# A routed feed-forward kernel: GpSimd retires its DMAs along the way, one expert's weights load later, and the planner's times change

## The chip, the cores and the metric

The kernel runs on one core of a Trainium2 chip. A core has five engines with their own instruction queues: TensorE (PE in the profile, with its weight loads as PEld), VectorE (DVE), ScalarE (ACT), GpSimd (POOL) and SyncE (SP). SP and ACT issue plain DMAs, on the profile's queues q1 and q10. GpSimd issues the indirect ones, gathers and scatters by a list of row numbers, on q0. All of them are carried out by the core's 16 DMA engines. The time is device microseconds of one execution. Before the change it was 445.34 us, the median of 3 runs (443.35 to 445.86).

## The reference

The inputs are `x` (8 batches of 256 tokens with 256 features), a context of 77 rows for each batch, and a mask.

```
h   = x + layernorm_affine(softmax(mask(LN(x) @ ctx^T / 16)) @ ctx)
out = h + sum over the two best of 8 experts e of
          p_e * ((silu(g_e) * u_e) @ w_down[e]),   [g_e, u_e] = LN(h) @ w_gate_up[e]
```

The two best experts of a token are those with the largest gate probability, `softmax(LN(h) @ w_gate)`, and the two probabilities are scaled to sum to 1. Everything is float32. One expert has 2 MB of gate and up weights (256 x 2048) and 1 MB of down weights (1024 x 256).

## The kernel before

**Two halves.** The first half handles the batches as eight *units* of 256 tokens: attention, the second layer norm, the choice of two experts. Each unit adds its result to `out` (line 816) and stores its normalized rows with gates and expert numbers into a scratch tensor in memory, `xn_rows` (line 850; unit 1 from SP's queue, the others from ACT's). After unit 1, and again after unit 2, a small table of row numbers is made (`first_table`). The second half goes over 29 *tiles* of tokens that belong to one expert (`tile_work`). Tiles 0 to 7 hold the first tokens of the experts 0 to 7, tile 0 from units 0 and 1, the others from units 0 to 2. Tiles 8 to 28 follow a second table and need all units; eight of them are wide, with two groups of rows.

**One tile.** GpSimd gathers the tile's rows from `xn_rows` into one of four buffers `xg` (line 1185, in `pool_rows`). PE transposes them (1264), ACT copies the result (1271), and PE multiplies with the gate and up weights (1314). ACT takes silu (1336), DVE the product (1343), and PE multiplies with the down weights (1375, or 1372 in a wide tile). DVE scales by the gate (1423), and GpSimd adds the rows to `out` with an accumulating scatter (1189). DVE also computes each token's gate from the gathered rows (1278, in `gate`), and the first of these works of tiles 0 and 1 matters below. Each scatter waits for the one before it to have landed. The last tile (28) is different: GpSimd reads the rows that `out` holds by then into `sums` (line 1185 again), DVE adds them in (1421), and the last scatter writes without accumulating.

**Weights.** Three buffers (`LANES = 3`) hold the weights of three experts. `weight_dmas` issues three DMAs on SP for one expert: two halves of `wgu` (line 259) and `wd` (260). The loop at line 284 issues those of experts 0 and 1 at the start of the kernel, behind the inputs. The load for tile 2 waits, through a one-element memset of its buffer (line 1234), for the gate work of tile 1. Later loads wait for the products that last used the buffer.

**The order.** The order on each engine's queue is written by a planner (`class Order`). Every piece of work is entered with an engine, a cost, what it needs, a rank, and a `lag`, the time from its end until others may use its result. The planner walks through time and emits, on each engine, the work that can begin first; among those within `NEAR` of each other it takes the lowest rank. An engine carries out its queue strictly in that order. Work with the engine "in" stands for inputs that arrive at a given time (`c_in`, `x_in`, `m_in_`, `gb_in`, lines 345 to 350). PE's work that begins before `WARM` is planned at 1.9 times its cost. Where the planner sees PE without work ahead of tile 0, it fills the gap with dummy products (`fill`, line 314, line 319 in the profile), at 0.22 us each before `WARM` and 0.12 after.

Of the kernel before, what the change touches and what calls it, by code (L numbers as in the profile page):

```python
# [33 lines left out]
class Order:  # L34
# [7 lines left out]
    LAG = {"pe": 0.12, "dve": 0.12, "act": 0.08, "pool": 0.10, "sp": 2.2, "in": 0.0}  # L42
    NEAR = 0.2

    WARM, COLD = 8.0, 1.9

    def __init__(self, bufs, fill=None):
        self.bufs = bufs
# [4 lines left out]
    def add(self, eng, cost, emit=None, needs=(), rank=0.0, lag=None, takes=(), uses=(), after=(), slack=0.0):  # L53
        lag = self.LAG[eng] if lag is None else lag
        w = Work(eng, cost, emit, list(needs), list(after), rank, lag, list(takes), slack)
        for b in list(takes) + list(uses):
            b.users.append(w)
        self.all.append(w)
        return w
# [61 lines left out]
def kernel(  # L121
# [36 lines left out]
    nc = tc.nc  # L158
    P = 128
    B, S, D = x.shape  # L160
# [10 lines left out]
    LANES = 3  # L171

    PARTS = [(2, 0, 1), (3, 1, E)]
    UF, UA = PARTS[0][0], PARTS[-1][0]
# [82 lines left out]
    def weight_dmas(l, gu, d, **kw):  # L257
        for up in range(2):
            nc.sync.dma_start(wgu[l][:, :, ts(up, F)], gu[:, :, ts(up, F)], **kw)
        nc.sync.dma_start(wd[l], d, **kw)  # L260

    def load_expert(l, e):
        weight_dmas(
            l,
            w_gate_up[e].rearrange("(c p) f -> p c f", p=P),
            w_down[e].rearrange("(c p) d -> p c d", p=P),
        )
# [13 lines left out]

    SWITCHED = [getattr(mybir.EngineType, e) for e in ("PE", "DVE", "Activation", "SP")]
    TURNED = 100
    for e in range(LANES - 1):
        load_expert(e, e)


    def iota(dst, pattern, base, mult):
# [34 lines left out]
    add = order.add  # L323
# [19 lines left out]


    c_in = [add("in", 0.0, lag=3.8 if b == 0 else 7.3 if b < UA else 14.0) for b in range(B)]
    x_in = [add("in", 0.0, lag=(4.4, 7.0, 10.0)[b] if b < UA else 16.0) for b in range(B)]
    m_in_ = [add("in", 0.0, lag=4.3 if b == 0 else 11.6 if b < UA else 19.4) for b in range(B)]
    wg_in = add("in", 0.0, lag=4.6)
    gbr_in = add("in", 0.0, lag=6.0)
    gb_in = add("in", 0.0, lag=10.7)  # L350


    cT = keep.tile([P, B, NC, CT + E], F32, name="cT")
# [78 lines left out]
    lists = keep.tile([P, P], F32, name="lists")  # L432
    routed, stored = [], []
    held_back = {}

    def unit(b):

        first, front = b == 0, b < UA
        r = 100.0 * b
# [11 lines left out]
        def dve(cost, emit, needs, k, **kw):  # L451
            return add("dve", cost, emit, needs, r + k, **kw)

        def pe(cost, emit, needs, k, **kw):

            return add("pe", cost, emit, needs, r + k, slack=0.0 if front else SLACK, **kw)
# [68 lines left out]
        if b > UA:  # L525
            tp.after.append(routed[UA - 1]["lists"])
        xT = add("act", 0.6, copy_x, [tp], r + 4, takes=[b_xT], uses=[b_tp])
        lps = pe(1.0, logits, [xT, c_c, *W], 5, takes=[b_lps], uses=[b_xT],
            after=[u["sub"] for u in routed[-1:]],
        )  # L530
# [47 lines left out]
        def masked():  # L578
# [8 lines left out]
        sub = dve(  # L587
            0.31,
            lambda: nc.vector.tensor_tensor(
                v["lg"], v["lg"], mx.unsqueeze(2).to_broadcast([P, NT, T]), ALU.subtract  # L590
            ),
            [m_x], 8, uses=[b_lg],
        )
# [15 lines left out]
        ex = add("act", 0.75 if front else 3.2, exps, [sub, r_q], r + 9, takes=[b_prob], uses=[b_lg])  # L609

        if b == UA:
            held_back.update(r_q=r_q, ex=ex)

# [55 lines left out]
        e12 = row[:, :, EXP : EXP + 2]  # L671
# [15 lines left out]
        e_12 = dve(0.09, lambda: nc.vector.tensor_copy(e12, i8[:, :, :2]), ix8, 17, takes=[b_row], after=[u["e12"] for u in routed[-1:]])  # L687
# [32 lines left out]
        cnt, dep = [], ([routed[-1]["cnt"]] if routed else [])  # L720
# [3 lines left out]
        rk = pe(0.3, ranks, [b_th, cnt[0], consts], 20, takes=[b_rk])  # L724
# [29 lines left out]
        def one_hots(i):  # L754
            j, k = divmod(i, 2)
            if i == 0:
                for n in ("oh_hi", "oh_lo"):
                    v[n] = work.tile([P, NP, P], F16, tag=n, name=f"{n}{b}")
            t = b * NT + j
            nc.vector.tensor_scalar(v["oh_hi"][:, i, :], iota_h, hi[:, j, k : k + 1], None, ALU.is_equal)  # L760
            nc.vector.tensor_scalar(
                v["oh_lo"][:, i, :], iota_h, lo[:, i : i + 1], number_of[:, t : t + 1], ALU.is_equal, ALU.mult
            )
# [15 lines left out]
        for i in range(NP):  # L779
            w = dve(  # L780
                0.38, lambda i=i: one_hots(i), [h_f, l_f, consts, *dep], 25 + 0.1 * i,
                takes=[b_oh] if i == 0 else [], uses=[] if i == 0 else [b_oh],
            )
# [3 lines left out]
        l_s = dve(  # L787
            0.29, to_lists, [ltp] + ([routed[-1]["lists"]] if routed else []), 27, uses=[b_ltp]
        )
# [40 lines left out]
        def normalize(j):  # L830
            nc.scalar.activation(
                row[:, j, :D], xb[:, j, :], AF.Identity, bias=nmr[:, j : j + 1], scale=rx[:, j : j + 1]
            )
# [3 lines left out]
        x_n = [add("act", 0.5, lambda j=j: normalize(j), [n_r, e_12], rs + 0.06, after=[t_h]) for j in range(NT)]  # L837
# [12 lines left out]
            eng, 0.45, lambda: q.dma_start(xn_t[:, tiles_b, :], row), [*x_n, e_12, *g_], rs + 0.08,  # L850
            lag=3.5, uses=[b_row],
        )
        routed.append({"counting": [cnt[0], rk], "lps": lps, "sub": sub, "e12": e_12, "cnt": cnt[-1], "lists": l_s})
        stored.append([o_1, s_n])

    for b in range(B):
# [308 lines left out]
    def load_weights(t):  # L1165
        f, m, l = tiles[t]
        if f == 0:
            return load_expert(l, m)
        kw = {}
        if f == 1:  # L1170
            kw = dict(cond=nc.sync.value_load(new[0:1, m : m + 1], min_val=0, max_val=1), cond_hint=False)
        weight_dmas(l, *weights_of(eid_w if f == 2 else eid, m), **kw)
# [7 lines left out]
    def pool_rows(t, at, tile_, in_=None, out_=None, **kw):  # L1180

        n = S * units_of(t)
        at = bass.IndirectOffsetOnAxis(ap=at, axis=0)
        if in_ is not None:
            nc.gpsimd.indirect_dma_start(  # L1185
                out=tile_, out_offset=None, in_=in_[:n], in_offset=at, bounds_check=n - 1, oob_is_err=False
            )
        else:
            nc.gpsimd.indirect_dma_start(  # L1189
                out=out_[:n], out_offset=at, in_=tile_, in_offset=None, bounds_check=n - 1, oob_is_err=False, **kw  # L1190
            )

    lane_last = {}
    count = []
    gathers, done = [], []
# [4 lines left out]
    def tile_work(t):  # L1200
# [18 lines left out]
        r, rp = -1000.0 + t, 1.0e6 + 100.0 * t  # L1219
        units = stored[: units_of(t)]  # L1220
        v = {}
        needs = list(ew)
        if l in lane_last:
            needs.append(lane_last[l])
        if t == MT0:
            needs.append(guessed)
        if t < LANES - 1:
            weights = add("in", 0.0, lag=40.0)
        elif f == 0:
            needs += [w for s in stored[:UF] for w in s] if t < LANES else []  # L1230
            if t == LANES - 1:

                needs.append(
                    add("dve", 0.08, lambda: nc.vector.memset(wgu[l][:1, 0, :1], 0.0), [held_back["gc"]], r)
                )
            weights = add("sp", 2.0, lambda: load_weights(t), needs, r, lag=8.0)
        else:
            weights = add("sp", 1.0, lambda: load_weights(t), needs, r, lag=8.0 if wide else 3.0)

        b_x, got, where = [], [], []  # L1240
        for n, at in groups:
# [3 lines left out]
            def gather(n=n, at=at, dst=where[-1]):  # L1245
                pool_rows(t, at, dst[:n], in_=xn_d)
                if t == MB - 1:
# [5 lines left out]
                    lag=3.0, takes=[b_x[-1]], after=gathers[-1:],  # L1253
# [39 lines left out]
        ]  # L1293


        if t == LANES - 2:
            held_back.update(gc=gc[0])

        b_hT = [Buf("hT") for _ in range(1 + wide)]
# [109 lines left out]
        if last:  # L1409

            read = add(
                "pool", 1.05, lambda: pool_rows(t, groups[0][1], sums, in_=out_rows), done[-1:], r, lag=3.0
            )

        def gated(i):
            n = groups[i][0]
            v["y", i] = hpool.tile([P, D], F32, tag="y", name=f"y{t}_{i}", bufs=3)
            src = v["rows"][:n, i, :] if turned else v["o", i][:n]
            gc = v["gc", i][:n, 0:1]
            if last:  # L1420
                nc.vector.scalar_tensor_tensor(v["y", i], src, gc, sums, ALU.mult, ALU.add)
            else:
                nc.vector.tensor_scalar(v["y", i][:n], src, gc, None, ALU.mult)  # L1423

        for i, (n, at) in enumerate(groups):
            y = add(
                "dve", 0.4, lambda i=i: gated(i), [rows[i], gc[i]] + ([read] if last else []), r, takes=[b_y[i]],
                uses=[b_r[i], b_gs[i]],
            )
            kw = {} if last else dict(compute_op=ALU.add)  # L1430
            done.append(
                add(
                    "pool", 1.58,
                    lambda i=i, n=n, at=at, kw=kw: pool_rows(t, at, v["y", i][:n], out_=out_rows, **kw),
                    [y] + [s[0] for s in units] + done[-1:], r, lag=6.0, uses=[b_y[i]],
                )
            )

    def rest_tile(m):

# [57 lines left out]
    for t in range(MB):  # L1498
        if t == MT0:
            guessed = add(  # L1500
                "sp", 3.0, lambda: load_expert(TURN1[0], HELD[0]), [lane_last[TURN1[0]]], -1000, lag=3.0
            )
        tile_work(t)
# [40 lines left out]
```

## Time and profile before

| | |
|---|---|
| three runs | 445.34, 445.86, 443.35 us |
| profiled execution: time, span of its instructions | 443.19, 441.5 us |
| mean granted clock of TensorE | 0.988 |
| PE busy | 424.8 us, 96% |
| PEld, DVE, ACT, POOL busy | 399.4, 150.8, 121.9, 131.8 us |
| gate and up products (line 1314) | 2 x 928, 268.0 us |
| down products (lines 1375 and 1372) | 592, 125.2 us |
| fillers (line 319) | 111, 17.1 us |
| gathers, scatters of GpSimd | 37 of 1.05 us, 37 of 1.55 us, and one read |
| DMA | 92.58 MB, mean 210 GB/s |

The page has a row for each engine with the span cut into 40 slices of 11 us; a digit is the busy share in tenths. `PEclk` is the clock that TensorE was granted. A timeline row gives start and duration in us, the engine, the line, the operation and its operands; the bracket at its end says how long the engine had been idle and what ended that. A `q` behind an engine's name marks its instruction queue, where DMAs are issued and semaphores are waited for. The semaphore of a DMA is full when the last of its 16 parts has landed, and the trace records that time.

### The profile page before, as it was taken

What the parts mean: (1) busy time and instruction counts of PE and PEld (TensorE: products, weight loads), DVE (VectorE), ACT (ScalarE), POOL (GpSimd) and SP (SyncE); (2) the same over time, 40 slices, a digit from 0 to 9 for tenths busy, and PEclk for the clock granted to TensorE, in tenths of its full rate; (3) what the DMA queues carried; (4) which work ended last, traced back from release to release, by engine and by line L of the source; (5) the groups of instructions that cost most, each with busy time, mean ns of one, the idle gap of its engine ahead of it and who ended that gap; (6) DMA issues with size and microseconds to landing.
All of it is one profiled execution on the core that took longest, in us unless ns stands there. A gap on an engine that the chain in (4) does not pass through costs nothing. (4 is left out here: it accounts for less than half of the span.)

```text
span 441.5 us, 8045 instructions
## 1 busy us (share of the span) xinstructions
PE 424.8 (96%) x2958; PEld 399.4 (90%) x2958; DVE 150.8 (34%) x679; ACT 121.9 (28%) x298; POOL 131.8 (30%) x155
## 2 busy tenths in 40 slices
PE   7997999999999999999999999999999999999991
PEld 5875999899999988998899989999999999999991
DVE  4597577777762111212111121111212212122210
ACT  6674777762311111111111101111111111111110
POOL 6663443322225320332023212313304224021220
PEclk9699999999999999999999999999999999999998
DMA  6994399999997993791479764658246178751110
GB/s 164 327 387 159 80 358 380 319 303 322 337 303 261 369 341 125 221 303 30 167 222 294 267 202 117 186 161 292 40 126 201 25 265 259 233 165 16 13 26 20
DMA packets 54531, 92.58 MB, mean 210 GB/s; under 512 B 5512, under 2 KB 41092, under 8 KB 54481
## 3 DMA queue, kind: packets, MB, share of 16 engines
q1 hardware_dynamic: 45356, 81.25, 53.9%
q0 software_dynamic: 6688, 8.59, 10.3%
q10 hardware_dynamic: 2437, 2.11, 1.4%
q8 instruction: 26, 0.43, 0.4%
q14 instruction: 24, 0.20, 0.1%
HBM read 102.69 MB, written 8.71 MB: 252 GB/s over the span
## 5 line engine op out<-in xcount | busy, mean ns | idle before, releaser
L1314 PE MATMUL g<-xgT,wgu 128*128 128x128 f32 (+8 forms) x928 | 134.1, 294 | 0.5 <-ACT xgT L1271 0.5
L1314 PE MATMUL u<-xgT,wgu 128*128 128x128 f32 (+8 forms) x928 | 133.9, 294 | 0.0
L1314 PEld LDWEIGHTS g<-xgT,wgu 128*128 128x128 f32 x928 | 123.2, 192 | 2.4 <-ACT xgT L1271 0.7
L1314 PEld LDWEIGHTS u<-xgT,wgu 128*128 128x128 f32 x928 | 123.5, 192 | 1.6
L1343 DVE TENSOR_TENSOR hT<-sil,u 128x512 f32<-128x512 f32 (+7 forms) x74 | 47.9, 647 | 167.1 <-PE u L1314 164.4
L1189 POOL DMA_INDIRECT out_dram<-y,idx x37 | 57.5, 1553 | 149.4 <-DVE gs L1278 78.2
L1375 PE MATMUL o<-wd,hT 128*128 128x256 f32 (+2 forms) x432 | 98.6, 380 | 0.0
L1375 PEld LDWEIGHTS o<-wd,hT 128*128 128x128 f32 (+2 forms) x432 | 79.8, 190 | 10.1
L1336 ACT ACTIVATE sil<-g 128x512 f32<-128x512 f32 (+7 forms) x74 | 41.8, 564 | 149.5 <-PE g L1314 146.0
L1185 POOL DMA_INDIRECT xg<-xn_rows,idx x37 | 38.8, 1049 | 106.8 <-PE tp L1264 91.0
L1271 ACT COPY xgT<-tp 128x256 f32<-128x256 f32 (+8 forms) x29 | 11.9, 410 | 102.3 <-PE tp L1264 102.1
L1423 DVE TENSOR_SCALAR y<-o,gc 128x256 f32<-128x256 f32 (+2 forms) x26 | 12.6, 484 | 54.0 <-PE o L1375 54.0
L1372 PE MATMUL o<-hT,wd 128*128 128x224 f32 (+4 forms) x160 | 26.6, 325 | 0.0
L1372 PEld LDWEIGHTS o<-hT,wd 128*128 128x128 f32 x160 | 25.9, 190 | 0.0
L319 PE MATMUL filled<-filler 128*128 128x256 bf16 x111 | 17.1, 297 | 1.2 <-DVE cT L387 1.2
L1264 PE MATMUL tp<-ident,xg 128*128 128x128 f32 (+7 forms) x74 | 12.8, 268 | 2.1 <-DMA xg<-xn_rows,idx 2.1
L1264 PEld LDWEIGHTS tp<-ident,xg 128*128 128x128 f32 (+7 forms) x74 | 9.7, 141 | 5.2 <-DMA xg<-xn_rows,idx 2.4
L319 PEld LDWEIGHTS <-filler 128*128 128x128 bf16 x111 | 11.1, 105 | 3.3 <-DVE cT L387 1.2
L1423 DVE TENSOR_SCALAR y<-rows,gc 128x256 f32<-128x256 f32 (+5 forms) x10 | 4.3, 476 | 28.4 <-PE rows L1404 28.4
L823 POOL TENSOR_TENSOR rx<-ss,neg_half 128x2 f32<-128x2 f32 x8 | 5.6, 699 | 19.7 <-DVE ss L820 19.3
L1392 ACT COPY oT<-o 128x224 f32<-128x224 f32 (+4 forms) x10 | 3.2, 317 | 28.2 <-PE o L1372 28.2
L635 PE MATMUL v<-av_w,pT 77*128 77x256 f32 x32 | 9.6, 426 | 0.8 <-ACT xT L513 0.8
(204 smaller groups left out, 308.5 us busy)
## 6 DMA issues: line engine op xcount, KB each, us to landing
wgu<-in_L_ffn_w_gate_up_dram SPq DMA_DIRECT2D x60, 1024.0 KB, 7.2
wd<-in_L_ffn_w_down_dram SPq DMA_DIRECT2D x30, 1024.0 KB, 8.2
out_dram<-x_all SPq DMA_DIRECT2D x8, 256.0 KB, 2.1
xn_rows<-xnr ACTq DMA_DIRECT2D x7, 260.0 KB
x_all<-in_x_dram SPq DMA_DIRECT2D x1, 1280.0 KB
x_all<-in_x_dram SPq DMA_DIRECT2D x3, 256.0 KB, 3.2
xg<-xn_rows,idx POOLq DMA_INDIRECT x37, 5.0
out_dram<-y,idx POOLq DMA_INDIRECT x37, 4.3
```

The lines of the kernel that those rows point to most:

```text
L319: nc.tensor.matmul(filled, filler[:, :P], filler, start=True, stop=True)
L635: nc.tensor.matmul(v["v"][:, j, :], v["pT"][:, j, :], av_w[:, b, KC:], start=True, stop=True)
L1185: nc.gpsimd.indirect_dma_start(out=tile_, out_offset=None, in_=in_[:n], in_offset=at, bounds_check=n - 1, oob_is_err=False)
L1189: nc.gpsimd.indirect_dma_start(out=out_[:n], out_offset=at, in_=tile_, in_offset=None, bounds_check=n - 1, oob_is_err=False, **kw)
L1264: nc.tensor.transpose(v["tp"][:, c, off : off + n], src[:n, ts(c, P)], ident[:n, :n])
L1271: nc.scalar.copy(v["xT"][:, :, :W], v["tp"][:, :, :W])
L1314: nc.tensor.matmul(v[tag, h][:, i, : W if wide else P], wgu[l][:, c, bass.ds(off + (h + i) * P, P)], v["xT"][:, c, : W if wide else P], st ...
L1336: nc.scalar.activation(v["sil", h], v["g", h][:, :, : min(W, per)], AF.Silu)
L1343: nc.vector.tensor_tensor(v["hT", h // held][:, bass.ds(h % held, FG), : min(W, per)], v["sil", h], v["u", h][:, :, : min(W, per)], ALU.mult,)
L1372: nc.tensor.matmul(v["o", d][:, :W], wd[l][:, i, ts(d, P)], hT[:, :W], **kw)
L1375: nc.tensor.matmul(v["o", d][:n], hT[:, offs[d] : offs[d] + n], wd[l][:, i, :], **kw)
L1423: nc.vector.tensor_scalar(v["y", i][:n], src, gc, None, ALU.mult)
```

## The change

There are three parts.

1. *Drains.* A new function enters a `drain` instruction on GpSimd, which holds GpSimd's queue until its outstanding DMAs are done. One stands after every fourth tile (tiles 3, 7, 11, 15, 19, 23 and 27), behind the landing of that tile's last scatter; one more stands in the last tile, behind the read into `sums`. The planner has 2.0 us for each.
2. *Weights.* Only expert 0's weights are issued at the start. Tile 1's load now waits like tile 2's: for a memset of its buffer that waits for the gate work of the tile before. Tile 2's load no longer names the stores of units 0 and 1 as something to wait for.
3. *The planner's figures.* `WARM` goes from 8.0 to 4.6, and four arrival times are lowered. Unit 3's exponentials are planned after the beginning of unit 2's normalization (`x_n`).

```diff
-    WARM, COLD = 8.0, 1.9
+    WARM, COLD = 4.6, 1.9
...
-    for e in range(LANES - 1):
-        load_expert(e, e)
+    load_expert(0, 0)
...
-    x_in = [add("in", 0.0, lag=(4.4, 7.0, 10.0)[b] if b < UA else 16.0) for b in range(B)]
-    m_in_ = [add("in", 0.0, lag=4.3 if b == 0 else 11.6 if b < UA else 19.4) for b in range(B)]
+    x_in = [add("in", 0.0, lag=(4.2, 7.0, 10.0)[b] if b < UA else 14.0) for b in range(B)]
+    m_in_ = [add("in", 0.0, lag=4.3 if b == 0 else 11.6 if b < UA else 17.0) for b in range(B)]
...
-    gb_in = add("in", 0.0, lag=10.7)
+    gb_in = add("in", 0.0, lag=10.3)
...
         if b == UA:
             held_back.update(r_q=r_q, ex=ex)
+            ex.after.extend(routed[-1]["x_n"])
...
-        routed.append({"counting": [cnt[0], rk], "lps": lps, "sub": sub, "e12": e_12, "cnt": cnt[-1], "lists": l_s})
+        routed.append({"counting": [cnt[0], rk], "lps": lps, "sub": sub, "e12": e_12, "cnt": cnt[-1], "lists": l_s, "x_n": x_n})
...
+    def drain(needs, r):
+
+        add("pool", 2.0, lambda: nc.gpsimd.drain(), needs, r)
...
-        if t < LANES - 1:
-            weights = add("in", 0.0, lag=40.0)
+        if t == 0:
+            weights = add("in", 0.0, lag=24.0)
         elif f == 0:
-            needs += [w for s in stored[:UF] for w in s] if t < LANES else []
-            if t == LANES - 1:
+            if t < LANES:
 
                 needs.append(
                     add("dve", 0.08, lambda: nc.vector.memset(wgu[l][:1, 0, :1], 0.0), [held_back["gc"]], r)
                 )
...
-        if t == LANES - 2:
+        if t < LANES - 1:
             held_back.update(gc=gc[0])
...
                 "pool", 1.05, lambda: pool_rows(t, groups[0][1], sums, in_=out_rows), done[-1:], r, lag=3.0
             )
+            drain([read], r)
...
+
+        if t % 4 == 3:
+            drain(done[-1:], r)
```

## The prediction

> **What bounds the kernel now.** I read the page first, its row of TensorE (PE) and of the granted clock by slices, then the timeline around the first expert tile, the DMA queues in short windows, and last the instructions of the exit line.
>
> ```profile
> PE   7997999999999999999999999999999999999991
> PEclk9699999999999999999999999999999999999998
> ```
>
> From slice 6 (about 55 us) to slice 39 PE is full. So the time is a front in which PE waits, a full stretch whose length is the work itself, and a tail. Only an earlier start of the full stretch, a hole torn into it, or a shorter tail moves the end. The timeline, where the first expert tile starts (start, duration, engine, line; in brackets the idle time before and who ended it):
>
> ```profile
> 33.34 0.37 SPq L850 DMA_DIRECT2D xn_rows<-xnr  x1
> 39.35 1.30 POOL L1185 DMA_INDIRECT xg<-xn_rows,idx  x1 [2.19 <-issue]
> 42.69 0.44 PE L1264 MATMUL tp<-ident,xg 128*128 128x128 f32 x2 [2.10 <-DMA xg<-xn_rows,idx]
> 44.64 0.40 ACTq L850 DMA_DIRECT2D xn_rows<-xnr  x1
> 48.05 1.09 POOL L1185 DMA_INDIRECT xg<-xn_rows,idx  x1 [5.95 <-DVE lists L941]
> ```
>
> Unit 1's rows are stored at 33.34, the first gather leaves at 39.35, PE waits 2.10 for it, and tile 0 starts. That store's semaphore is full only at 38.46 by the trace: 5.1 us. Unit 2's, issued at 44.64, is full at 47.26: 2.6 us. The windows 34 to 36 and 42 to 46 us say why (queue: packets, MB, share of the 16 DMA engines):
>
> ```profile
> q1 hardware_dynamic: 762, 0.74, 109.1%
> ...
> q10 hardware_dynamic: 141, 0.15, 10.6%
> ```
>
> At 34 us SP's queue q1 is still full, with expert 1's weights (landed 30.5, 33.4 and 36.2) and two output stores ahead of the rows; at 42 to 46 us the wire is free. Last the tail, the exit line and the final timeline rows:
>
> ```profile
> 426.96 1.08 POOL L1185 DMA_INDIRECT sums<-out_dram,idx  x1 [2.58 <-DMA out_dram<-y,idx]
> 432.65 0.48 DVE L1421 SCALAR_TENSOR_TENSOR y<-o,gc,sums 128x256 f32<-128x256 f32 x1 [2.70 <-PE o L1375]
> 433.41 1.03 POOL L1189 DMA_INDIRECT out_dram<-y,idx  x1 [5.38 <-DVE y L1421]
> ...
> L1539 POOLq DRAIN  x3: 46/107/7001, 433.7 to 441.2; - x3
> L1539 SPq DRAIN  x3: 7/7/7, 437.6 to 440.9; - x3
> ```
>
> The last scatter has landed at 437.0 and SP passes its exit waits at 437.6, but GpSimd's exit drain lasts 7.00 us, to 440.65, and the end follows 0.8 later. Its two later drains, with nothing outstanding, take 0.11 and 0.05.
>
> **The change, part by part.** The profiled execution took 443.19 (span 441.5). The runs are 443.35, 445.34 and 445.86; with the profiled one their mean is 444.4, and I add my sum to that, 0.9 below the median 445.34.
>
> *Exit drain, -3.0.* Before, 75 GpSimd DMAs (37 gathers, 37 scatters, one read) are retired by one drain. Between the end of the last scatter on GpSimd (434.44) and the drain's end lie 6.2 us, 0.083 per DMA if it is a price per DMA. After, at most the last scatter is outstanding, and the drain should end with the landing at 437.1. Then SP's 437.67 is what ends last, and the end comes at 437.67 + 0.8 = 438.47 in place of 441.47. Bounds: nothing (a fixed 3.65 after the landing, 440.65 - 437.0) to -3.0. I take -3.0, since the nearest rows, the two drains without outstanding DMAs, cost next to nothing.
>
> *Seven drains in the middle and one in the last tile, 0.* Bounds of one: 0.05 to 7.0. Each is placed on the planner's time after its scatter has landed. After tiles 11, 15, 19 and 23 GpSimd idles 14.4, 8.0, 14.2 and 12.9 us before its next work, after tile 7's gathers 6.4, after tile 3 5.5 before unit 7's `rx`, and that unit's rows are needed only by gathers at 131. Behind a drain wait scatters and gathers for tiles whose buffers were freed early; 3.65 is hidden everywhere. The two at the end are not so free: the drain of tile 27 stands ahead of the read of `sums` (426.96), the last tile's behind it. The sums land at 430.70, `y` is ready at 433.13: 2.43 us for both together. By 0.083 a DMA, six outstanding and then one, they cost 0.6, so nothing on the path.
>
> *Expert 1's weights leave the front, -2.05.* Three of six weight DMAs go from SP's start. The wire is full from 10 to 36 us and 3.1 MB at the 385 GB/s of 20 to 34 us are 8 us of it, so by 33.34 it is empty, and unit 1's store should take unit 2's 2.6: full at 35.96. GpSimd then has its `ry` and `av_w` ahead of the gather, to 37.17; the gather leaves at 37.3 in place of 39.35 and tile 0 starts 2.05 earlier. Bounds: 0 (the queue position moves with the plan) to -2.5 (without `av_w` ahead). PE's work ahead of it is fillers from 37.7 on, so the start moves one to one.
>
> *The same weights behind the first gathered rows, +2.0.* The memset after tile 0's gate releases the three DMAs about 0.4 after tile 0's rows (call that time T). Expert 2's set, issued at 53.39 into an emptier wire, landed at 60.1, 63.1 and 66.6, so 6.7, 9.7 and 13.2 later. Tile 1's first product comes at T + 15.6 (58.30), so the weights themselves are in time by some 5 us. What is late next is unit 2's row store on ACT's queue, at T + 2.0: it now meets a full wire. The six stores of before that met one took 8.0, 7.4, 6.3, 6.1, 6.7 and 6.1, against 2.6. So it is full at T + 8.1 to 10.0, tile 1's gather leaves 0.8 later (47.26 to 48.05) and lands 3.0 after that (48.05 to 51.05): T + 11.9 to 13.8. PE, in order, comes to tile 1's transposes at T + 10.4 (53.10). It would stand 1.5 to 3.4 us. Expert 2's weights moved their first packets 1.1 after the issue and filled the wire (share 0.99) only 2.6 after it, so at T + 2.0 the wire is filling, not full: I take 2.0, near the lower end. Bounds: 0 to 4.
>
> [...]
>
> *The planner's clock guard and arrival times, -1.2.* They alter the order written out and the number of fillers, and no row shows the new order. Two rows bound the gain: PE waits 1.17 for `bw`, which DVE has queued behind an addition that waits for beta until 9.90; and the clock is 0.50 from 11.3 to 18.1 us, which makes unit 1's eight logits products 1.84 in place of 1.02. With PE no longer thought slow from 4.6 to 8 us, `bw` is due about a microsecond earlier and ahead of that addition. So -1.2, with -3 (the clock dip goes as well) and +1.5 (an order that fits worse) as bounds.
>
> [...]
>
> *The added order on ACT*, unit 3's exponentials after unit 2's normalization: already so in the trace (normalization 43.53, exponentials 48.28): 0, at most 0.5 either way.
>
> Sum: -3.0 - 2.05 + 2.0 - 1.2 = -4.25, so 444.4 - 4.25 = 440.15; for the profiled execution 438.9.
>
> **The rivals.**
> 1. *No hole at tile 1.* If the store slips in while the wire fills, the 2.0 go: -6.25, 438.15. For it: the wire is full at T + 3.0, and unit 2's store of before had moved its first packets 0.9 after its issue, so at T + 2.9. Against it: none of six loaded stores took under 6.1.
> 2. *Slower: a drain has a fixed price after landing.* Place: the two drains around the read of the sums. Price: 3.65 each. The drain of tile 27 moves the read from 426.96 to 430.6, the sums land at 434.35, the second drain ends at 438.0 and the last scatter leaves at 438.3, not 433.41: +4.85, and the exit drain stays 7.0. With the front's -1.25 that is +3.6, 448.0. It decides from 2.4 us for the two together. Against it: the drains of 0.05 and 0.11.
> 3. *The exit drain stays as it is* although the drains inside cost little, because its tail belongs to the last DMA: only the front's -1.25 is left, 443.15.
>
> **How the numbers follow.** A run of this kernel scatters so that 0.5% (2.2 us) is about what can be told from no change. Forecast 440.15: 0.42. Rival 1: 0.20. Rival 2: 0.13. Rival 3: 0.17. Something worse in the front (the order, weights late): 0.08. Faster, below 443.1: nearly all of the forecast (0.40), rival 1 and half of rival 3, 0.68. Slower, over 447.6: two thirds of rival 2 and a little of the last, 0.11. Within 0.5%: the rest, 0.21. The range reaches from a little past rival 1 (437.0) over rival 3 with 2 us of scatter (446.0) and leaves rival 2 and what is worse in the front out, some 0.2 in all.
>
> **What the profile would show.** The exit drain of GpSimd down from 7.0 to about 3.5, and ended with the last landing; drains in the middle of 0.5 to 2 us in idle time; the last scatter still some 0.8 us after PE's last product. The store of unit 1 full within 3 us, the first gather about 2 us earlier. A wait of PE at line 1264 for `xg` at tile 1, 1.5 to 3.4 us, with unit 2's store taking over 6. PE's `bw` wait gone. I am wrong if drains take over 2.4 us together at the end, if the new order delays unit 1's store, or if tile 1 waits for weights at line 1314.

## The result, and the profile after

The changed kernel takes 448.91 us (448.72 to 449.52, 6 runs) against 445.29 (443.35 to 445.86, 6 runs) of the kernel before: 1.0091 of its time, 95% interval 1.0072 to 1.0110. It is slower by about 4 us, where 440.2, a gain of some 4 us, was forecast. The profiled execution took 449.16, its span is 447.4 (443.19 and 441.5 before).

The two rows of the page that the prediction began with, now of the kernel after:

```profile
PE   8889799999999799999999999999999999999995
PEclk9999959999999999999999999999999999999998
```

PE is no longer full from slice 6 on (slice 14 has a 7), and the clock has a hole in slice 6, about 56 to 67 us. Cut in the prediction's three pieces, from the two traces (us):

| | before | after | difference |
|---|---|---|---|
| front: tile 0's first gate product starts | 43.58 | 41.26 | -2.32 |
| full stretch: from there to PE's last product | 389.02 | 400.76 | +11.74 |
| tail: from there to the end of the span | 8.86 | 5.42 | -3.44 |

The tail gave what was forecast, the front most of it. The full stretch lost 11.7 us. Waits of PE over 0.25 us in it add up to 6.86 (0.85 before), 6.0 more. From 55.9 to 66.2, 10.2 us, the granted clock is 0.50. The first 0.9 of these lie inside one of the waits; the other 9.3 lose about half of their work, by estimate some 4.7 us. Together that is 10.7 of the 11.7.

The timeline of the kernel after, SP, ACT, GpSimd and PE around tiles 0 and 1:

```profile
32.51 0.37 SPq L850 DMA_DIRECT2D xn_rows<-xnr  x1
37.14 1.32 POOL L1185 DMA_INDIRECT xg<-xn_rows,idx  x1 [1.28 <-DVE vy L659]
40.36 0.44 PE L1267 MATMUL tp<-ident,xg 128*128 128x128 f32 x2 [0.34 <-DMA xg<-xn_rows,idx]
41.05 0.89 SPq L259 DMA_DIRECT2D wgu<-in_L_ffn_w_gate_up_dram  x2
45.98 0.40 ACTq L850 DMA_DIRECT2D xn_rows<-xnr  x1
53.93 1.08 POOL L1185 DMA_INDIRECT xg<-xn_rows,idx  x1 [9.99 <-DMA xn_rows<-xnr]
56.82 0.69 PE L1267 MATMUL tp<-ident,xg 128*128 128x128 f32 x2 [2.96 <-DMA xg<-xn_rows,idx]
57.02 0.89 SPq L259 DMA_DIRECT2D wgu<-in_L_ffn_w_gate_up_dram  x2
```

Unit 1's store, with the wire empty, is full at 36.2, 3.7 after its issue, and PE's wait for tile 0's rows is down from 2.10 to 0.34. Then expert 1's weights go out at 41.05, unit 2's rows at 45.98. Those rows are full only at 53.1. GpSimd stands idle 9.99 us until they are (5.95 before), the gather leaves at 53.93, and PE, which had come to tile 1's transposes at 53.9, waits 2.96. The queues of the same trace in the windows 46 to 48 and 50 to 53 us (packets, MB, share of the 16 DMA engines):

```profile
q1 hardware_dynamic: 203, 0.82, 102.6%
...
q1 hardware_dynamic: 791, 0.79, 80.8%
q10 hardware_dynamic: 258, 0.25, 24.0%
```

In the 2 us after its issue the store, on ACT's queue q10, moved no packet at all; SP's queue had the whole wire (102.6%). Its first packet moved 3.6 us after the issue, and nearly all of its packets (258 of 272) went between 50 and 53 us. In the kernel before, unit 0's store, issued at 24.47, which also met weights, moved its first packet 3.7 us after the issue, at 28.2, and unit 2's, on an empty wire, 0.9. What holds back the first packet on a loaded wire is not shown here.

Once the store's packets moved, SP's queue kept most of the wire: from 50 to 53 us q1 had 80.8% of the engines' time and q10 24.0%. In the kernel before, from 29 to 31 us beside unit 0's store, it was 80.1% and 23.8%, with 163 packets of about 4 KB on q1 and 160 of about 1 KB on q10. These shares do not account for the late start.

What the late gather does next shows in three more stretches of the trace. The windows from 54 to 62 us (us, busy time of PE, PEld, DVE, ACT and POOL with instruction counts, granted clock, DMA share, GB/s):

```profile
54.00:56.00 2.00, 0.00 (x0) 0.00 (x0) 0.00 (x0) 0.00 (x0) 1.70 (x2) 0.98 0.17 46
...
58.00:60.00 2.00, 2.00 (x8) 1.73 (x8) 0.56 (x3) 0.00 (x0) 1.69 (x2) 0.50 0.76 219
60.00:62.00 2.00, 2.00 (x7) 1.53 (x6) 0.25 (x2) 0.00 (x0) 1.70 (x2) 0.50 1.01 361
```

PE stands for two microseconds, and when it starts again the clock is 0.50. PE is then counted busy, but with 7 or 8 instructions in 2 us (19 in the window from 66 to 68, with the clock at 0.96). The second stretch is where the second table's first tiles start:

```profile
141.38 0.21 DVE L1149 TENSOR_SCALAR idx<-ids 128x48 int32<-128x48 f32 x1 [1.12 <-PE ids L1145]
...
151.50 0.22 DVE L1281 SCALAR_TENSOR_TENSOR gs<-xg,em_w 128x2 f32<-128x2 f32 x1 [6.50 <-DMA xg<-xn_rows,idx]
152.39 1.99 PE L1378 MATMUL o<-wd,hT 128*128 128x256 f32 x8 [1.89 <-DVE hT L1346]
155.46 1.99 PE L1378 MATMUL o<-wd,hT 128*128 128x256 f32 x8 [1.08 <-DVE hT L1346]
```

The table's row numbers are ready at 141.4, where they were at 130.7 before. The gathers that wait for them are that much later, DVE, in order, stands 6.50 us at the gate work of one of them, the `hT` behind it is late, and PE waits 1.89 and 1.08. Last the end, drains among it (count, then shortest/median/longest in ns, first and last start):

```profile
437.23 1.08 POOL L1185 DMA_INDIRECT sums<-out_dram,idx  x1 [3.44 <-issue]
442.06 0.48 DVE L1425 SCALAR_TENSOR_TENSOR y<-o,gc,sums 128x256 f32<-128x256 f32 x1 [2.70 <-PE o L1378]
442.82 1.03 POOL L1189 DMA_INDIRECT out_dram<-y,idx  x1 [4.50 <-DVE y L1425]
...
L1195 POOLq DRAIN  x8: 3341/5324/8524, 112.5 to 437.0; - x8
L1546 POOLq DRAIN  x3: 46/108/3272, 442.8 to 447.2; - x3
```

The exit drain takes 3.27 in place of 7.00 and ends at 446.04, 0.07 after the last landing (445.97). The eight new drains are long in the list, 3.3 to 8.5 us, but they start while scatters or gathers are still in flight, and end soon after the last of these has landed (0.08 to 0.55 us in `e1_drains` below, whose trace gives every landing). That they cost PE nothing is shown there too. The last scatter leaves 0.76 after `y` begins, as before.

### The profile page after: what moved, and what is told of

It is laid out like the page before. It is cut to its first block, busy times and chain, and to the rows that moved or that the text cites. A ratio compares the mean times of both kernels' runs of the same rounds, so it can differ in the third digit from the quotient of the medians.

```text
span 447.4 us, 8059 instructions
## 1 busy us (share of the span) xinstructions
PE 428.0 (96%) x2962; PEld 400.4 (89%) x2962; DVE 150.6 (34%) x680; ACT 121.8 (27%) x298; POOL 132.6 (30%) x155
## 5 line engine op out<-in xcount | busy, mean ns | idle before, releaser
L1317 PE MATMUL g<-xgT,wgu 128*128 128x128 f32 (+8 forms) x928 | 135.5, 296 | 0.5 <-ACT xgT L1274 0.5
L1317 PEld LDWEIGHTS g<-xgT,wgu 128*128 128x128 f32 x928 | 124.7, 194 | 2.4 <-ACT xgT L1274 0.7
L1378 PE MATMUL o<-wd,hT 128*128 128x256 f32 (+2 forms) x432 | 100.5, 383 | 3.0 <-DVE hT L1346 3.0
L318 PEld LDWEIGHTS <-filler 128*128 128x128 bf16 x115 | 11.3, 105 | 3.1 <-DVE cT L386 1.2
L1395 ACT COPY oT<-o 128x224 f32<-128x224 f32 (+4 forms) x10 | 3.2, 318 | 28.2 <-PE o L1375 28.2
L761 DVE TENSOR_SCALAR oh_lo<-iota_h,lo,number_of 128x128 f16<-128x128 f16 x32 | 9.8, 307 | 0.0
```

Of the source, the lines that this page charges most:

```text
L318: nc.tensor.matmul(filled, filler[:, :P], filler, start=True, stop=True)
L761: nc.vector.tensor_scalar(v["oh_lo"][:, i, :], iota_h, lo[:, i : i + 1], number_of[:, t : t + 1], ALU.is_equal, ALU.mult)
L1317: nc.tensor.matmul(v[tag, h][:, i, : W if wide else P], wgu[l][:, c, bass.ds(off + (h + i) * P, P)], v["xT"][:, c, : W if wide else P], st ...
L1378: nc.tensor.matmul(v["o", d][:n], hT[:, offs[d] : offs[d] + n], wd[l][:, i, :], **kw)
```

## The experiments

Three theories. A: expert 1's weights share the wire with unit 2's row store, and that is the loss. B: the drains hold GpSimd. C: the new figures lead the planner to a worse order. Every ratio below is to the kernel before on the same chip; the microseconds in brackets are that ratio times the kernel before there (443.9 to 446.6).

### Each part alone, and the two others without the weights

`e1_drains`, part 1 alone:

```diff
+    def drain(needs, r):
+        add("pool", 2.0, lambda: nc.gpsimd.drain(), needs, r)
...
+            drain([read], r)
...
+        if t % 4 == 3:
+            drain(done[-1:], r)
```

> The kernel before with part 1 alone: GpSimd's drains at every fourth tile and in the last tile. Theory A (the weights of expert 1, on the wire while unit 2's rows are stored, are the whole loss; a drain only pays for what is outstanding, about 0.05 us per DMA after the last landing): the exit drain ends 0.1 us after the last landing in place of 3.65, PE's last product to the end 5.4 us in place of 8.9, PE's stretch unchanged: 3.5 us faster, 441.8. Theory B (the drains inside, 3.3 to 8.5 us each in the changed kernel, hold GpSimd's work and make PE wait): PE's stretch longer by 3 us or more, so 445 or above. Theory C (the loss is the planner's new order): as A here.

Measured: 440.27, ratio 0.9903 (0.9864 to 0.9941; -4.3 us). Faster than both kernels. Its drains, then those of the exit:

```profile
L1195 POOLq DRAIN  x8: 3280/5037/8729, 107.4 to 430.2; - x8
L1547 POOLq DRAIN  x3: 46/108/3471, 435.9 to 440.5; - x3
```

The tail is 5.62 in place of 8.86, and PE's waits over 0.25 us in the full stretch add up to 0.85, as in the kernel before. B falls.

`e2_weights`, part 2 alone:

```diff
-    for e in range(LANES - 1):
-        load_expert(e, e)
+    load_expert(0, 0)
...
-            needs += [w for s in stored[:UF] for w in s] if t < LANES else []
-            if t == LANES - 1:
+            if t < LANES:
...
```

> The kernel before with part 2 alone: expert 1's weights behind tile 0's gate, with the planner's old figures and no drains. Theory A: tile 0 starts some 2 us earlier, unit 2's store takes about 7 us, PE waits about 3 us for tile 1's rows, the granted clock falls to 0.50 for one stretch of 7 to 10 us behind that (3.5 to 4.7 us lost), and the held GpSimd makes the second table later: 4 to 8 us slower, 449 to 453. Theory B and C: nothing but the earlier start, about 443.3.

Measured: 448.78, ratio 1.0115 (1.0069 to 1.0162; +5.1). Its timeline:

```profile
40.79 0.89 SPq L259 DMA_DIRECT2D wgu<-in_L_ffn_w_gate_up_dram  x2
42.57 0.40 ACTq L849 DMA_DIRECT2D xn_rows<-xnr  x1
54.62 0.44 PE L1262 MATMUL tp<-ident,xg 128*128 128x128 f32 x2 [3.43 <-DMA xg<-xn_rows,idx]
```

Tile 0's first product starts at 41.51, 2.07 earlier than before. The store, 1.8 after the weights, is full 8.3 later (2.6 before); PE waits 3.43, and the clock is 0.50 for 6.8 us after it. That is A's chain, without the drains and with the old figures. A new plan is no part of it: in the two traces PE, ACT and GpSimd carry out the same instructions in the same order; DVE has one memset more, and on SP the three loads have moved.

`e3_planner`, part 3 alone:

```diff
-    WARM, COLD = 8.0, 1.9
+    WARM, COLD = 4.6, 1.9
...
-    x_in = [add("in", 0.0, lag=(4.4, 7.0, 10.0)[b] if b < UA else 16.0) for b in range(B)]
-    m_in_ = [add("in", 0.0, lag=4.3 if b == 0 else 11.6 if b < UA else 19.4) for b in range(B)]
+    x_in = [add("in", 0.0, lag=(4.2, 7.0, 10.0)[b] if b < UA else 14.0) for b in range(B)]
+    m_in_ = [add("in", 0.0, lag=4.3 if b == 0 else 11.6 if b < UA else 17.0) for b in range(B)]
...
-    gb_in = add("in", 0.0, lag=10.7)
+    gb_in = add("in", 0.0, lag=10.3)
...
+            ex.after.extend(routed[-1]["x_n"])
```

> The kernel before with part 3 alone: the planner's clock guard, arrival times and the added order on ACT. Theory A: unit 1's rows are stored 0.8 us earlier, but behind the same weights, no half-clock stretch at 11 to 18 us, tile 0 at most 1 us earlier: 444.5, between 443.5 and 446. Theory C: the new order puts GpSimd's work for units 3 to 7 behind the gathers and scatters, units late, and PE waits at the second table: 448 or more. Theory B: as A.

Measured: 449.29, ratio 1.0125 (1.0084 to 1.0166; +5.6). C holds as well: the planner's figures alone cost about as much as the whole change does.

`e4_no_weights`, parts 1 and 3:

> The changed kernel without part 2: drains and the planner's new figures, with the weights of experts 0 and 1 both at the start. Theory A: all of the loss is gone and the drains' gain stays: 441 (3.5 from the exit drain, 0.8 from the front), so 7 to 8 us below the changed kernel's 448.9. Theory B or C: it stays within 2 us of 448.9.

Measured: 444.65, ratio 1.0010 (0.9991 to 1.0030; +0.4). Neither forecast fits it, that of A (441) or that of C (446.9 or more): each theory has a part of the loss. Part 2 on top of it, which is the changed kernel, costs 0.8% more. The three single parts sum to -4.3 + 5.1 + 5.6 = +6.4, the changed kernel has +4.0. An overlap of some 2 us would fit with parts 2 and 3 both delaying unit 2's rows, but the three intervals together leave the sum some 3 us of room either way, so the overlap is not shown.

### Does the halved clock cost its length?

`e5_fill_hole` keeps PE busy while it waits at tile 1:

```diff
+            if t == 1:
+                for _ in range(26):
+                    nc.tensor.matmul(
+                        v["tp"].rearrange("p c k -> p (c k)"), filler[:, :P], filler, start=True, stop=True
+                    )
```

> The changed kernel with 26 idle products on PE ahead of tile 1's transposes, into the PSUM tile that the transposes then overwrite. It asks what the hole at tile 1 costs beyond its own length. If the clock falls because PE stands (the granted clock of the changed kernel is 0.50 for 10.2 us right after the 2.96 us hole), the hole of tile 1's first real product stays at about 3 us, the clock stays at 1, and the time is 4.5 to 5 us lower: about 444.2. If the clock falls for another reason, the time stays at 448.9 or rises by the part of the idle products that outlasts the wait (0 to 1 us). The later holes of about 1.9 and 1.1 us near 150 us belong to GpSimd's 10 us wait and should stay in both cases.

Measured: 451.03, ratio 1.0147 (1.0081 to 1.0212; +6.5): no gain, and against the changed kernel (1.0072 to 1.0110) no difference outside the intervals. The timeline of PE, and of DVE at the same time:

```profile
54.07 3.00 PE L1267 MATMUL tp<-filler 128*128 128x256 bf16 x26
57.60 0.44 PE L1272 MATMUL tp<-ident,xg 128*128 128x128 f32 x2 [0.52 <-DMA xg<-xn_rows,idx]
66.43 1.09 PE L518 MATMUL lps<-cT,xT 128*128 128x86 f32 x8 [3.32 <-DVE v L682]
```

```profile
65.85 0.16 DVE L1286 SCALAR_TENSOR_TENSOR gs<-xg 128x2 f32<-128x2 f32 x1 [2.18 <-DMA xg<-xn_rows,idx]
66.20 0.29 DVE L682 MAX8 v<-gl 128x8 f32<-128x8 f32 x2
```

The wait is filled, and no clock dip follows it: from there the clock holds until 67.6. But PE, with the clock at 1, comes early to unit 3's logits (line 518) and waits 3.32 us there, by the trace for DVE at line 682. DVE stands, in order, at gate work for rows that were gathered after tile 1's. These gathers left at 56 to 60, as late as tile 1's made them, and so some of them beside expert 2's weights (issued 57.80), and they landed up to 66.7. Then a dip of 3.4 us follows that wait. So in this trace another wait stands where the half clock of the changed kernel was; its 5 us are not a term that can be taken off by itself. Both go back to the late row store, which GpSimd's gathers waited for.

### Is there a better place for the weights?

Both kernels have the drains and the old figures. `e9_drains_store1` issues expert 1's weights right behind unit 1's row store on SP, `e10_drains_store2` behind unit 2's, with that store moved to SP:

```diff
+            if t == 1:
+                needs += [w for s in stored[:UF] for w in s]
+            elif t < LANES:
```

```diff
-        q, eng = (nc.sync, "sp") if b == UF - 1 else (nc.scalar, "act")
+        q, eng = (nc.sync, "sp") if b in (UF - 1, UA - 1) else (nc.scalar, "act")
...
+            if t == 1:
+                needs.append(stored[UA - 1][1])
+            elif t < LANES:
```

> The kernel before with part 1 (all drains), and with expert 1's weights taken from the front of SP's queue and put behind unit 1's row store in the same queue, without the wait for tile 0's rows; the planner's figures as before. If the loss of part 2 lies in the weights meeting unit 2's row store on the wire, issuing them some 7 us earlier keeps the early start of tile 0 (some 2 us before 43.6) and has no hole at tile 1: 440.3 for the drains alone minus 2, about 438.3, range 436.5 to 440.3. If the weights behind unit 1's store slow that store or the first gather, tile 0 starts no earlier and the time is that of the drains alone, 440.3, or up to 3 above it.

> The same, but with the weights behind unit 2's row store in SP's queue (that store moved from ACT's queue to SP's). Both of the first row stores have an empty wire. If the conflict is only with that store, there is no hole at tile 1's transposes, tile 0 starts some 2 us earlier than in the kernel before, and the time is 438 to 440. The weights are then the late ones: if they land over 10 us after tile 1's rows, PE waits for them at tile 1's gate and up products and the time is 441 to 444.

Measured: 0.9982 (0.9950 to 1.0013; -0.8) and 0.9992 (0.9958 to 1.0026; -0.4), so about as the kernel before, and 3.5 to 4 us slower than the drains alone. The timelines say why, first `e9_drains_store1`, then `e10_drains_store2`:

```profile
35.90 1.00 SPq L259 DMA_DIRECT2D wgu<-in_L_ffn_w_gate_up_dram  x2
39.50 1.30 POOL L1184 DMA_INDIRECT xg<-xn_rows,idx  x1 [0.19 <-POOL av_w L478]
45.93 0.69 PE L1268 MATMUL tp<-ident,xg 128*128 128x128 f32 x2 [3.21 <-DMA xg<-xn_rows,idx]
```

```profile
43.63 1.00 SPq L259 DMA_DIRECT2D wgu<-in_L_ffn_w_gate_up_dram  x2
46.85 1.09 POOL L1184 DMA_INDIRECT xg<-xn_rows,idx  x1 [5.24 <-DMA xn_rows<-xnr]
53.97 0.44 PE L1268 MATMUL tp<-ident,xg 128*128 128x128 f32 x2 [2.13 <-DMA xg<-xn_rows,idx]
```

The first two row stores that the gathers wait for, those of units 1 and 2, are quick now (2.7 to 2.9), but in the first kernel tile 0's gather meets the weights and lands 6.4 after its issue (3.3 before), and tile 0's gate products start at 47.08; in the second it is tile 1's gather, 7.1 in place of 3.0. The edits spared the stores, and not the gathers. With the places of the two kernels that are the subject here, that makes four: at the start (unit 1's store takes 5.1, against 2.6 to 3.7 in the kernels without them there; 4.4 to 6.5 in the others with them), behind unit 1's store (tile 0's gather), behind tile 0's rows (unit 2's store), behind unit 2's store (tile 1's gather). Each one meets a transfer that the next tile waits for. Of the three with the drains and the old figures (`e1_drains`, `e9_drains_store1`, `e10_drains_store2`) the start costs least.

### Which of the planner's figures?

`e11_warm` has the clock guard alone, `e12_arrivals` the four arrival times alone, `e16_numbers_only` both without the added order on ACT. (By itself the added order changes no engine's instruction order.)

> The kernel before with the clock guard's start alone (WARM 8.0 to 4.6). All of part 3 by itself cost some 4.8 us. If this number makes the bad order, the time is 447 to 450, the later part of unit 3's work (the products of its ranks or its transposes) waits in holes of over 1 us, and unit 2's rows are stored some 5 us after tile 0's first product. If the arrival times make it, the time is 444.4 and unit 2's normalization still stands ahead of tile 0's first silu, as in the kernel before.

> The kernel before with the four arrival times alone. If they make the bad order, the time is 447 to 450 with holes as in the run of all of part 3; if the clock guard makes it, 444.4. If each does a part, both runs lie at 446 to 447; if only the two together do, both stay at 444.4.

> The clock guard's start and the arrival times together, without the added order on ACT (unit 3's exponentials after unit 2's normalization). Each number alone moved nothing; all of part 3 cost 4.8 us. If the two numbers together make the loss, the time is 447 to 450, with unit 2's rows stored some 6 us after tile 0's first product. If the loss needs the added order, the time is 444 to 445.

Measured: 1.0013 (0.9993 to 1.0033), 0.9989 (0.9967 to 1.0011) and 1.0141 (1.0083 to 1.0198; +6.3). Each number moves nothing, the two together make the loss, and the added order does not make it.

`e14_planner_norm_first` is all of part 3 with one order put back on ACT:

```diff
             sl = add("act", 0.6, silu, accs["g"][1], r, takes=[b_sil], uses=[accs["g"][0]])
+            if t == 0 and h == 0:
+                sl.after.extend(routed[UA - 1]["x_n"])
```

> All of part 3, and tile 0's first silu (with its table load) put behind unit 2's normalization on ACT, as it stands in the kernel before; the rest of ACT's order is unchanged. With part 3 alone ACT stood 1.66 us at that silu for PE's products while unit 2's rows, behind it, were stored only at 50.7. If that order on ACT is what part 3 lost, unit 2's store leaves some 2 us earlier and the time falls from 449.3 to 445 to 447. If the loss is in PE's order (products of unit 3's ranks ahead of tile 0's gate products, 1.1 us of hole and the clock that falls after it), the store comes earlier but the time stays at 449 within 1 us.

Measured: 446.49, ratio 1.0070 (1.0045 to 1.0094; +3.1). The timelines, `e3_planner` first, then `e14_planner_norm_first`:

```profile
44.88 0.17 PE L717 MATMUL rk<-both,tri 128*128 128x8 bf16 x1 [1.09 <-DVE both L700]
48.96 0.60 ACT L1337 ACTIVATE sil<-g 128x512 f32<-128x512 f32 x1 [1.66 <-PE g L1315]
49.55 1.08 ACT L832 ACTIVATE xnr<-x_all,nmr,rx 128x256 f32<-128x256 f32 x2
50.66 0.40 ACTq L851 DMA_DIRECT2D xn_rows<-xnr  x1
```

```profile
44.03 0.17 PE L717 MATMUL rk<-both,tri 128*128 128x8 bf16 x1 [1.11 <-DVE both L700]
46.55 1.08 ACT L832 ACTIVATE xnr<-x_all,nmr,rx 128x256 f32<-128x256 f32 x2
48.06 0.40 ACTq L851 DMA_DIRECT2D xn_rows<-xnr  x1
48.94 0.60 ACT L1337 ACTIVATE sil<-g 128x512 f32<-128x512 f32 x1
```

In `e3_planner` ACT stands 1.66 at tile 0's silu with unit 2's normalization behind it. With the two exchanged, the store leaves 2.6 earlier, 1.8 of it against the start of tile 0, and the time falls by some 2.5 us (0.3 to 4.6 by the two intervals). What is left, 3.1, has in the trace the ranks `rk` ahead of tile 0's gate products (1.1 of wait), the squares of unit 2 still behind tile 0's copy, and waits of 0.64 and 0.49 later. The kernels with the weights at the start go roughly by one number, the distance from tile 0's first gate product to the issue of unit 2's row store:

| | distance, us | cost against before, us |
|---|---|---|
| before, `e11_warm`, `e12_arrivals` | 1.1 each | 0, +0.6, -0.5 |
| `e14_planner_norm_first` | 3.7 | +3.1 |
| `e4_no_weights`, against `e1_drains` | 3.8 | +4.8 |
| `e3_planner` | 5.5 | +5.6 |
| `e16_numbers_only` | 8.6 | +6.3 |

`e4_no_weights` has the front's order of `e3_planner`, so its 3.8 beside that one's 5.5 is how far two executions of one order differ. It is a correlation over six orders, three of which share one distance, with one trace of each kernel; `e14_planner_norm_first` is the one edit that moved the store on purpose, and it took back about half. So that the late store makes a part of the loss is shown; what the rest consists of stays open.

### What the drains retire

`e8_one_drain` is the kernel before with a single drain after tile 15 (`if t == 15: drain(done[-1:], r)`).

> The kernel before with a single drain of GpSimd after tile 15 and nothing else. It asks what the exit drain's length counts. If it is a price per DMA issued on GpSimd since the last drain (about 0.047 us each from the drains of the runs so far), the drain after tile 15 ends 1.5 to 1.8 us after the landing of its last scatter, and the exit drain ends 1.8 to 2.1 us after the last landing in place of 3.65, so the end comes some 1.7 us earlier: about 443.6. If it is fixed for any drain with scatters behind it, both are 3.65, and the time is that of before. If it belongs to the whole run of the queue, the exit drain keeps 3.65 and the one in the middle takes half of it.

Measured: 442.91, ratio 0.9949 (0.9914 to 0.9984; -2.3). The drain and the exit line:

```profile
L1195 POOLq DRAIN  x1: 6204/6204/6204, 268.0 to 268.0; - x1
...
L1546 POOLq DRAIN  x3: 46/108/4778, 435.9 to 441.3; - x3
```

GpSimd had issued 44 DMAs ahead of the drain in the middle and 31 more ahead of the exit (the last scatter ahead of each starts just after the start that the trace gives the drain, which stands in the queue). The first ends 1.85 after the landing of the last of them, the second 1.31. With the 75 of the kernel before (3.65) and drains of `e1_drains` over 11, 6 and 1 (0.49, 0.28, 0.07) all lie between 0.04 and 0.05 us for each DMA, 0.07 for a single one. The exit was over-expected (1.8 to 2.1) because I had not counted the DMAs on either side.

### The wait at tile 0

`e17_drains_fill0` is `e1_drains` with 18 idle products ahead of tile 0's transposes, in the manner of `e5_fill_hole`.

> The kernel before with the drains, and 18 idle products on PE (about 0.115 us each, 2.1 in all) ahead of tile 0's transposes, in the wait for the first gathered rows. In the runs of this front the granted clock fell to 0.50 for 3.4 us or more right after a wait of 2.2 to 3.3 us there. If PE's wait there makes it fall, the wait shrinks to about 0.6 us, the clock stays at 1 after 41 us, and the time is 1.5 to 2 us under that of the drains alone (440.3): 438.4 to 438.8. If something else makes it fall, or if the work behind it was waiting anyway, the time stays at 440.3 within 1 us.

Measured: 441.13, on a chip where the kernel before took 446.60: ratio 0.9897 (0.9853 to 0.9940), against 0.9903 (0.9864 to 0.9941) of the drains alone. The granted clock of `e1_drains`, then of `e17_drains_fill0`:

```profile
PEclk9999899999999999999999999999999999999999
```

```profile
PEclk9999999999999999999999999999999999999998
```

The wait shrinks from 2.69 to 0.96 and the dip of 3.4 us at 44.5 is gone. A gain of 1.5 to 2 us does not show in the ratios, whose intervals are 3.4 and 3.9 us wide, so whether that dip was worth anything stays open. Of all the kernels run, `e1_drains` is the simplest of the two fastest.

## Why the prediction was wrong

*Exit drain, -3.0: right.* The tail fell by 3.24 in `e1_drains` and 3.44 in the changed kernel, and the drain ends with the landing (0.07 us after it). The price per DMA was put too high (0.083; 0.04 to 0.05 measured), because I counted the flight of the last scatter as price. The ratio of `e1_drains` says -4.3, with -3.2 inside its interval (-2.6 to -6.0).

*Eight drains inside, 0: right.* Nothing in the tail waits for them, and `e1_drains` is faster by the tail. Rivals 2 (a fixed price) and 3 (the exit stays) are both refuted. One reading was wrong: they last 3.3 to 8.5 us, not 0.5 to 2, because each starts before its scatter or read has landed, not after.

*Weights leave the front, -2.05: right.* 2.32 in the changed kernel, 2.07 in `e2_weights`, each from one trace. With the order of the kernel before in the front, tile 0 started at 43.58, 44.24 (`e8_one_drain`) and 44.48 (`e1_drains`), so the gain may be up to a microsecond larger.

*Weights behind tile 0's rows, +2.0: the wait right, what follows it missing.* The step had worked out 1.5 to 3.4 by the six loaded stores and then taken the lower end, since "the wire is filling, not full". The store fared as on a full wire: its first packet moved 3.6 and 3.9 us after the issue, it took 7.1 and 8.3, and PE waited 2.96 and 3.43. That is the smaller error. The term ended at that wait, as if PE had nothing else to lose. The same late rows held GpSimd 9.99 us, so the gathers behind tile 1's met expert 2's weights, the clock was 0.50 for 10.2 us from within the wait on (55.9), the later units and the second table came later, and with the old figures the move costs +5.1 (3.1 to 7.2) where the two terms said about 0. My bounds of 0 to 4 for this one term would have had to reach 7. The prediction asked of this stall only "what is late next" for tile 1, not for the units that share its engines.

*Planner's figures, -1.2: the step that failed most.* Part 3 alone measures +5.6 (3.7 to 7.4), outside my bounds of -3 and +1.5. In its place the runs show that the new order stores unit 2's rows 5.5 us after tile 0's first gate product (3.8 in `e4_no_weights`, of the same order), where the order of before had 1.1; putting ACT's order back there took off 2.5 of the 5.6, and the cause of the other 3.1 stays open. Of the two rows that bounded the term, the wait near 10 us did shrink (0.45 in the changed kernel, though one of 1.68 at 16.3 took its place), and the clock dip between 11 and 18 us does not come with the order alone: `e1_drains`, with the order of before there, has none and still starts tile 0 at 44.48, later than the kernel before with the dip (43.58). Neither shows in the start of tile 0, which is set by unit 1's store and the gather behind it; I had written that PE's work there "is fillers" and then still let its gain through. And I bounded a new order on five engines by two rows of the old one. Neither figure alone does harm (`e11_warm`, `e12_arrivals`), so no row of before could have priced the two together; a bound had to come from the slack of what the order may delay. Unit 2's rows had little: before, tile 1's gather left 0.8 us after their landing, and its rows lay ready 2 us when PE came to them.

*The added order on ACT, 0.* By itself no instruction moves, and the loss is there without it.

The sum has no single culprit: parts 2 and 3 each cost about as much as part 1 gives, or more (5.1 and 5.6 against 4.3), and both delay unit 2's rows. "Something worse in the front" had a chance of 0.08; it should have been the first rival.

## What to carry to other kernels

Ask of each transfer that is moved which small transfer it now stands next to, and follow that one through every engine that waits in order, not only to the first wait of PE: here four places for the same 3 MB each delayed a row store or a gather that the next tile needed. A gain ahead of a start that a DMA releases showed no worth here. A change of a planner's inputs is a change of order everywhere: its bound is the slack of the work on the path, not the waits one hopes to close.

## What the runs showed of the hardware

- In these traces GpSimd's drain ended after the last landing by 0.04 to 0.05 us for each DMA that GpSimd had issued since its last drain: 3.65 us for 75 (before), 1.85 for 44 and 1.31 for 31 (`e8_one_drain`), 0.49 for 11 and 0.28 for 6 (`e1_drains`, and the same in the changed kernel); for a single one it was 0.07 to 0.08. With eight drains ahead of the exit, the exit drain took 3.47 (`e1_drains`) in place of 7.00.
- The granted clock was 0.50 in stretches of 3.4, 6.8 or 10.2 us, mostly from within or shortly after a wait of PE: 10.2 at a wait of 2.96 (changed kernel), 6.8 at 3.43 (`e2_weights`), 6.8 at 2.13 (`e10_drains_store2`), 3.4 at 2.69 (`e1_drains`), none at 2.45 (`e4_no_weights`, mean clock 0.997) or 2.10 (before). The kernel before also has 0.50 for 6.8 us from 11.3, where no wait of PE is over 1.2, and `e1_drains`, with the same order there, does not. What makes the clock fall, and why it fell after a wait of 2.13 and not after one of 2.45, no run here settles.
- A small store on ACT's queue took 7.1 us (changed kernel) and 8.3 (`e2_weights`) beside weights on SP's, against 2.6 with an empty wire (before). Its first packet moved 3.6 and 3.9 us after the issue (2.7 to 3.7 in the six loaded stores of before on that queue, 0.9 with an empty wire). While both queues moved, the store's had 24.0% of the engines' time (changed kernel, 50 to 53 us) and 23.8% (before, 29 to 31 us).
